# Newton steps of a Stieltjes attention: two-input operations to GpSimd, one-input sums on VectorE

## The chip, the cores and the metric

One Trainium2 chip; the kernel runs on one of its cores. A core has five engines that run their own instruction streams: TensorE (PE; its weight loads are listed apart as PEld), VectorE (DVE), ScalarE (ACT), GpSimd (POOL) and SyncE (SP, which here issues the transfers). They wait for each other through semaphores. SBUF is the working memory of 128 partitions, PSUM the memory that TensorE writes. The metric is the device time of one execution in microseconds (us), lower is better; times are medians over executions.

## The reference

The input x is 8 sequences of 512 tokens of width 128. There are two parts, each behind a layer norm.

**Part A** is one causal "Stieltjes" attention with 16 heads of 8 channels. With scores s of one query row, it looks for the number lam at which the sum over the allowed keys of 1 / (lam - s) is 1, by four Newton steps:

```python
lam = s_masked.max(-1) + 1.0
for _ in range(num_iter):                     # 4
    d = jnp.maximum(lam[..., None] - s, EPS)
    w = jnp.where(mask, d ** (-q), 0.0)       # q = 1
    f = w.sum(-1) - 1.0
    fp = -q * jnp.where(mask, d ** (-q - 1.0), 0.0).sum(-1)
    lam = lam - f / fp
```

The weights 1 / (lam - s), divided by their sum, then weigh the values, and an output projection and the residual follow.

**Part B** is six layers. Each has a local attention (16 heads of 64 channels, windows of 32 tokens that also see the window before) and a gated feed-forward. Queries and keys are divided by their norm, `t / max(norm(t), 1e-12)`, scaled and rotated; the feed-forward starts with a layer norm. Each works on x with half of its channels shifted by one token.

## The kernel before, in words

**Part A** works on batches: one sequence and four of the 16 heads at a time, so 32 batches. `project` (L198) fetches x, normalizes and transposes it (`normalized_T`, L176; the scaled subtraction of each 128x128 block is L188) and forms queries, keys and values. `mask_q` (L238) multiplies the 128x512 queries by a per-partition mask that leaves the heads of the batch. `scores` (L242) leaves minus the scores in SBUF (tile `ns`, four row blocks, each in four pieces whose lengths are 32 to 512 keys: 16 columns of row state altogether), and their minimum in `mn`. `first_lam` (L266) makes the opening value from the minimum. A Newton step is then made of:

- `add_lam` (L261, L264): for the two short row blocks GpSimd adds lam to the negated scores. For the two long ones ScalarE does that inside its logarithm (L281).
- `evaluate` (L272): ScalarE forms 1/d as exp(-ln d); VectorE takes the statistics of each piece by `bn_stats` (L284), which leaves a count, a mean and a sum of squared deviations for each of two halves of the piece, in the tile `st` (128 x 16 x 2 x 3).
- `step` (L286): from these 96 numbers per partition, seven VectorE instructions of 16 to 64 columns compute the sum of w, the sum of w squared, and the new lam (L290 to L299):

```python
nc.vector.tensor_tensor(s1, mean, st[:, :, :, 0], ALU.mult)
nc.vector.tensor_tensor(q2, s1, mean, ALU.mult)
nc.vector.tensor_reduce(sw2, st[:, :, :, 0:3:2], axis=AX.XY, op=ALU.add)
nc.vector.scalar_tensor_tensor(sw, s1[:, :, 0], -1.0, s1[:, :, 1], ALU.add, ALU.add)
nc.vector.reciprocal(sw2, sw2)
nc.vector.tensor_tensor(sw, sw, sw2, ALU.mult)
nc.vector.scalar_tensor_tensor(lam, sw, 0.0, lam, ALU.max, ALU.add)
```

While one batch makes its four steps, the one before is weighed and summed (`attend_weigh`, `attend_sum`, `attend_end`) and the next one's scores are made. `stieltjes` (L360) hands out this work in quarters of a step: 464 quarters for the 7 sequences of the main stream. One sequence runs in a second stream with pools of its own, beside the first five batches of the main one. When a sequence is done, `sequence_end` (L346) fetches x again into a tile `xb`, adds, and writes to a scratch tensor x2; `enter` (L438) fetches that, normalizes and transposes it for part B. All three fetches use the tile name `xb`, with two buffers.

**Part B** walks through 48 units (layer, sequence), each in 8 slots of a pair of heads, so 384 slots (loop at L870). In each slot, `prepare_qk` (L594), one quarter ahead, projects queries and keys for two row blocks (L599), squares them on ScalarE (L605), multiplies by the rotation tables on VectorE (`qr`, L608), sums the squares (L614), adds the halves on GpSimd (L616), clamps the 128x16 sums from below (L622), turns them into 1/norm on ScalarE (L623, L624) and scales on GpSimd (L627). `prepare_v` makes the values, `spread` moves them by transfers on SP's queue (L652 to L657). `turn` transposes (L665, copied by ScalarE at L670), `weigh` makes the scores and takes off the row maximum (L684 to L695), `exponentials`, `turn_weights`, `gather` (L719, L728), `turn_sums` and `leave` finish the attention some slots later. `feed_forward` (L759) is a generator that advances by one piece per slot (by four in the first two sequences); its layer norm scales four 128x128 blocks at L778.

Part B starts after five batches of part A. From then on the loop also advances part A, by 1.65 quarters per slot (L930 to L932), until part A is done; the last 40% of the slots have part B alone.

The program is written in a language layer that derives every semaphore wait from the tiles that an instruction reads and writes. It fixes each engine's order of instructions before the run, with the written order as the priority and its own estimate of when inputs are ready; so on an engine, instructions of both parts are interleaved and not always in written order. At run time each engine works through its list in order.

Of the kernel before, what the change touches and what calls it, by code (L numbers as in the profile page):

```python
# [9 lines left out]
F32 = mybir.dt.float32  # L10
BF16 = mybir.dt.bfloat16
AF = mybir.ActivationFunctionType
ALU = mybir.AluOpType
# [37 lines left out]
def tile_kernel(  # L51
# [112 lines left out]

    STEPS = 4 * NUM_ITER

    def streams(pools, bank1):

        ns_p, dp, tr, pj, sm = pools

        def fetch(src):
            xb = pj.tile([P, NT, D], F32, name="xb", bufs=2)
            nc.sync.dma_start(xb, src.rearrange("(c p) d -> p c d", p=P))
            return xb

        def normalized_T(xb, dst):  # L176
            st = sm.tile([P, NT, 6], F32, name="st")
            mv = sm.tile([P, NT, 2], F32, name="mv")
            for c in range(NT):
                nc.vector.bn_stats(st[:, c, :], xb[:, c, :])  # L180
                nc.vector.bn_aggr(mv[:, c, :], st[:, c, :])
            rstd = sm.tile([P, NT], F32, name="rstd")
            nc.scalar.activation(rstd, mv[:, :, 1], AF.Ln, bias=eps_ln)
            nc.scalar.activation(rstd, rstd, AF.Exp, scale=-0.5)
            xn = pj.tile([P, NT, D], F32, name="xn", tag="xn")
            pt = bank1([P, N], "pt")
            for c in range(NT):
                nc.vector.tensor_scalar(  # L188
                    xn[:, c, :], xb[:, c, :], mv[:, c, 0:1], rstd[:, c : c + 1],
                    ALU.subtract, ALU.mult,  # L190
                )
# [27 lines left out]
            )  # L219
            return qs, kn, va  # L220

        def keys(rb, a):
            return (rb + 1) * P - Q * (3 - a)
# [13 lines left out]

        def mask_q(t):  # L238
            t["qj"] = qj = pj.tile([P, N], F32, name="qj")
            nc.vector.tensor_scalar(qj, t["proj"][0], jmask[:, t["j"] : t["j"] + 1], None, ALU.mult)  # L240

        def scores(t, rb):  # L242
            kn, qj = t["proj"][1], t["qj"]
# [21 lines left out]

        def first_lam(t):  # L266
            lam, mn = t["lam"], t["mn"]
            nc.vector.tensor_scalar(lam, mn, -1.0, 1.0, ALU.mult, ALU.add)
            for e in (2.0**-21, -(2.0**-21)):
                nc.vector.scalar_tensor_tensor(lam, mn, -1.0 - e, lam, ALU.mult, ALU.max)  # L270

        def evaluate(t, rb):  # L272
            ns, lam = t["ns"][rb], t["lam"]
# [11 lines left out]

        def step(t):  # L286
            st, lam = t["st"], t["lam"]
            mean = st[:, :, :, 1]
            s1 = sm.tile([P, H, 2], F32, name="s1")
            nc.vector.tensor_tensor(s1, mean, st[:, :, :, 0], ALU.mult)  # L290
            q2 = st[:, :, :, 0]
            nc.vector.tensor_tensor(q2, s1, mean, ALU.mult)
            sw2 = sm.tile([P, H], F32, name="sw2")
            nc.vector.tensor_reduce(sw2, st[:, :, :, 0:3:2], axis=AX.XY, op=ALU.add)
            sw = sm.tile([P, H], F32, name="sw")
            nc.vector.scalar_tensor_tensor(sw, s1[:, :, 0], -1.0, s1[:, :, 1], ALU.add, ALU.add)
            nc.vector.reciprocal(sw2, sw2)
            nc.vector.tensor_tensor(sw, sw, sw2, ALU.mult)
            nc.vector.scalar_tensor_tensor(lam, sw, 0.0, lam, ALU.max, ALU.add)  # L299

        def attend_weigh(t, rb):
            d = t["ns"][rb]
# [57 lines left out]
        def stieltjes(seqs):  # L360

            work = [(b, j) for b in seqs for j in range(4)]
            state = {}

            def open_batch(w):
                b, j = work[w]
                if j == 0:
                    state["proj"] = project(b)
                    state["o"] = pj.tile([P, NT, H, DH], F32, name="o")
                t = batch(b, j, state["proj"], state["o"])  # L370
                mask_q(t)
                return t

            now = open_batch(0)
            for rb in (3, 2, 1, 0):
                scores(now, rb)
            before = None
            for w in range(len(work) + 1):
                nxt = None
                if now:  # L380
                    first_lam(now)
                for k in range(NUM_ITER):
                    if now:
                        now["st"] = sm.tile([P, H, 2, 3], F32, name="stw")
                        now["df"] = {}
                        for rb in (1, 0):
                            now["df"][rb] = d = dp.tile([P, width(rb)], F32, name=f"df{rb}", bufs=1)
# [12 lines left out]
                    if now:  # L400
                        evaluate(now, 2)
                    if before and k == 0:
                        attend_weigh(before, 3)
                    if k == 0 and w + 1 < len(work):
                        nxt = open_batch(w + 1)
                    yield
                    if now:
                        evaluate(now, 1)
                    if before and k in (1, 2):
                        attend_sum(before, 4 - k)  # L410
                    if before and k == 1:
# [12 lines left out]
                before, now = now, nxt  # L424
# [144 lines left out]
        nc.gpsimd.tensor_copy(xs[hf:D, 1:N], xT[b][hf:D, 0 : N - 1])  # L569
        return xs  # L570

    turns = {"n": 0}

    def bank(shape, name):
        if done_steps >= (4 * NB + 1) * STEPS:
# [8 lines left out]
    for v in vst:  # L584
        nc.gpsimd.memset(v.rearrange("p c e h d -> p (c e h) d")[:, :, DHL:], 1.0)

    marks = {"act": None}

    def begin(u, qt, xs):
# [4 lines left out]
    def prepare_qk(g, wqkv, tab, cs):  # L594
        xs, q0 = g["xs"], (g["qt"] % 2) * HQ * DHL
        ss = ep.tile([P, 2, 2 * HQ], F32, name="ss", bufs=3)
        for i, c in enumerate(cs):
            m = bank([P, 2, HQ, DHL], "m")
            nc.tensor.matmul(  # L599
                m.rearrange("p t h e -> p t (h e)"), lhsT=xs[:, c * P : (c + 1) * P],  # L600
                rhs=wqkv[:, 0:2, q0 : q0 + HQ * DHL], start=True, stop=True,
            )
            qr = ep.tile([P, 2, 2, HQ, DHL], F32, name="qr")
            sq = ep.tile([P, 2 * HQ, DHL], F32, name="sq", bufs=1)
            marks["act"] = nc.scalar.activation(  # L605
                sq, m.rearrange("p t h e -> p (t h) e"), AF.Square
            )
            nc.vector.tensor_tensor(  # L608
                qr, m.unsqueeze(1).to_broadcast([P, 2, 2, HQ, DHL]),
                tab[:, i].rearrange("p (k t) e -> p k t e", k=2).unsqueeze(3).to_broadcast(  # L610
                    [P, 2, 2, HQ, DHL]
                ), ALU.mult,
            )
            nc.vector.tensor_reduce(ss[:, i, :], sq, axis=AX.X, op=ALU.add)  # L614
            halves_of = qr.rearrange("p k t h (u e) -> p k (t h) u e", u=2)
            nc.gpsimd.tensor_tensor(  # L616
                g["qn"][:, c].rearrange("p t h (u e) -> p (t h) u e", u=2),
                halves_of[:, 0], halves_of[:, 1, :, ::-1, :], ALU.add,
            )
        gelus()  # L620

        nc.vector.tensor_scalar(ss, ss, 1e-24, None, ALU.max)  # L622
# [136 lines left out]
    def feed_forward(u, w1, w2):  # L759
# [15 lines left out]
        nc.scalar.activation(rn, mv[:, :, 1], AF.Ln, bias=eps_ln)  # L775
        nc.scalar.activation(rn, rn, AF.Exp, scale=-0.5)
        for c in range(NT):
            nc.vector.tensor_scalar(  # L778
                xt[:, c, :], xt[:, c, :], mv[:, c, 0:1], rn[:, c : c + 1],
                ALU.subtract, ALU.mult,  # L780
            )
# [202 lines left out]
```

## Time and profile before

| | |
|---|---|
| median of 3 executions | 4896.63 us (4894.68 to 4904.67) |
| profiled execution | 4896.56 us, span 4894.9 us |
| instructions | 165932 |
| PE busy | 4172.2 us (85%) |
| DVE busy | 4155.8 us (85%) |
| ACT busy | 3517.7 us (72%) |
| POOL busy | 2990.9 us (61%) |
| granted TensorE clock, mean | 0.938 |

The profile is of one execution, by the hardware's own records; the span is from its first to its last instruction. "L12" is line 12 of the kernel. A group is a set of instructions of one line and shape, with its count, its busy time and the mean duration of one (ns); then follows how long its engine sat idle just before, and on what. In the answer for a single line, three numbers stand for the minimum, median and maximum duration in ns. In a timeline each row gives the start, the duration, the engine, the line and what is written from what; equal neighbours are merged, with their count. A wait is given as the waiting engine and line, the releaser, the total us, how often, and the longest. In a table of stretches, each engine's busy time stands in the order PE, PEld, DVE, ACT, POOL, followed by the granted clock of TensorE, the DMA share and GB/s.

### The profile page before, as it was taken

What the parts mean: (1) busy time and instruction counts of PE and PEld (TensorE: products, weight loads), DVE (VectorE), ACT (ScalarE), POOL (GpSimd) and SP (SyncE); (2) the same over time, 40 slices, a digit from 0 to 9 for tenths busy, and PEclk for the clock granted to TensorE, in tenths of its full rate; (3) what the DMA queues carried; (4) which work ended last, traced back from release to release, by engine and by line L of the source; (5) the groups of instructions that cost most, each with busy time, mean ns of one, the idle gap of its engine ahead of it and who ended that gap; (6) DMA issues with size and microseconds to landing.
All of it is one profiled execution on the core that took longest, in us unless ns stands there. A gap on an engine that the chain in (4) does not pass through costs nothing. (4 is left out here: it accounts for less than half of the span.)

```text
span 4894.9 us, 165932 instructions
## 1 busy us (share of the span) xinstructions
PE 4172.2 (85%) x68749; PEld 2525.4 (52%) x68749; DVE 4155.8 (85%) x9460; ACT 3517.7 (72%) x6298; POOL 2990.9 (61%) x3822
## 2 busy tenths in 40 slices
PE   4555788888888888898888888888999999999998
PEld 1232455544555454554555555555566666666664
DVE  8787888988999989988889999898787777777775
ACT  6898777777777777766777777777566666666664
POOL 3543666656566655666666665666566666666763
PEclk7666899999999999999999999999999999999999
DMA  1000222222222222222222222222233333333332
GB/s 47 1 1 26 52 65 52 62 59 54 59 54 69 61 56 46 65 59 46 63 53 57 53 48 67 47 55 59 65 89 79 80 87 71 85 73 83 85 72 57
DMA packets 558914, 288.89 MB, mean 59 GB/s; under 512 B 97580, under 2 KB 541264, under 8 KB 558160
## 3 DMA queue, kind: packets, MB, share of 16 engines
q1 hardware_dynamic: 558160, 278.26, 24.4%
q8 instruction: 543, 8.90, 0.8%
q14 instruction: 211, 1.73, 0.1%
HBM read 66.21 MB, written 7.34 MB: 15 GB/s over the span
## 5 line engine op out<-in xcount | busy, mean ns | idle before, releaser
L616 POOL TENSOR_TENSOR qn<-qr 128x512 f32<-128x512 f32 x768 | 979.1, 1275 | 1157.1 <-DVE qr L608 1128.4
L608 DVE TENSOR_TENSOR qr<-m,tab 128x1024 f32<-128x1024 f32 x768 | 935.6, 1218 | 293.8 <-ACT sq L605 245.9
L627 POOL TENSOR_TENSOR qn<-qn,ss 128x512 f32<-128x512 f32 x768 | 785.5, 1043 | 113.5 <-ACT ss L624 91.4
L599 PE MATMUL m<-wqkv,xs 128*128 128x512 f32 x1536 | 767.4, 616 | 54.9 <-ACT qT L670 43.8
L281 ACT ACTIVATE d<-ns,lam 128x416 f32<-128x416 f32 (+7 forms) x1024 | 577.8, 623 | 138.4 <-DVE lam L299 103.2
L605 ACT ACTIVATE sq<-m 128x512 f32<-128x512 f32 x768 | 459.1, 598 | 261.9 <-DVE ss L614 180.6
L264 POOL TENSOR_TENSOR df<-ns,lam 128x160 f32<-128x160 f32 (+7 forms) x1024 | 400.6, 427 | 330.5 <-DVE lam L299 207.7
L284 DVE BATCH_NORM_STATS2 stw<-d 128x6 f32<-128x416 f32 (+7 forms) x1024 | 520.5, 561 | 95.7 <-ACT d L282 94.5
L670 ACT COPY qT<-ptq 128x512 f32<-128x512 f32 x768 | 426.4, 586 | 167.2 <-PE ptq L665 165.2
L614 DVE TENSOR_REDUCE ss<-sq 128x8 f32<-128x512 f32 x768 | 517.5, 674 | 0.0
L636 PE MATMUL pv<-wqkv,xs 128*128 128x256 f32 x1536 | 450.1, 416 | 58.4 <-DVE qr L608 43.7
L665 PEld LDWEIGHTS ptq<-ident,qn 128*128 128x128 f32 x3072 | 356.1, 143 | 255.7 <-issue 91.4
L665 PE MATMUL ptq<-ident,qn 128*128 128x128 f32 x3072 | 454.6, 282 | 38.7 <-ACT v L639 22.1
L695 POOL TENSOR_TENSOR pr<-pr,nm 128x512 f32<-128x512 f32 x384 | 400.2, 1042 | 68.7 <-DVE nm L694 57.0
L316 PE MATMUL dTp<-ident,ns 128*128 128x128 f32 x1280 | 245.4, 314 | 224.1 <-ACT ns L304 134.2
L740 ACT COPY oT<-po 128x512 f32<-128x512 f32 x384 | 224.5, 585 | 283.8 <-PE po L736 283.5
L252 PE MATMUL s<-kn,qj 32*32 32x224 f32 (+15 forms) x4096 | 365.7, 430 | 71.3 <-DVE mn L256 59.0
L744 PE MATMUL acc<-oT,wo 128*128 128x512 f32 x768 | 402.2, 606 | 2.7 <-ACT oT L740 2.7
L719 PE MATMUL po<-v,prT 64*32 64x65 f32 x24576 | 393.7, 226 | 6.8 <-DVE pr L689 6.6
L599 PEld LDWEIGHTS m<-wqkv,xs 128*128 128x128 f32 x1536 | 265.4, 197 | 255.2 <-issue 121.3
L282 ACT ACTIVATE d<-d 128x1856 f32<-128x1856 f32 (+1 forms) x256 | 393.0, 1535 | 0.0
L719 PEld LDWEIGHTS po<-v,prT 64*32 64x32 f32 x24576 | 289.8, 106 | 167.4 <-issue 107.2
(135 smaller groups left out, 8118.3 us busy)
## 6 DMA issues: line engine op xcount, KB each, us to landing
v<-v SPq DMA_DIRECT2D x2304, 65.0 KB
v<-v SPq DMA_DIRECT2D x768, 48.8 KB
wqkv<-in_L_ffn_Wqkv_dram SPq DMA_DIRECT2D x72, 256.0 KB
v<-v SPq DMA_DIRECT2D x384, 32.5 KB
wqkv<-in_L_ffn_Wqkv_dram SPq DMA_DIRECT2D x72, 128.0 KB
wo<-in_L_ffn_Wo_dram SPq DMA_DIRECT2D x36, 256.0 KB
tab<-tabs SPq DMA_DIRECT2D x36, 256.0 KB
w<-in_L_ffn_W_dram SPq DMA_DIRECT2D x18, 341.0 KB
```

Source lines behind the costliest of these rows:

```text
L281: nc.scalar.activation(o, n, AF.Ln, bias=lam[:, c : c + 1])
L284: nc.vector.bn_stats(t["st"][:, 4 * rb + a].rearrange("p u k -> p (u k)"), o)
L599: nc.tensor.matmul(m.rearrange("p t h e -> p t (h e)"), lhsT=xs[:, c * P : (c + 1) * P], rhs=wqkv[:, 0:2, q0 : q0 + HQ * DHL], start=True, ...
L605: marks["act"] = nc.scalar.activation(sq, m.rearrange("p t h e -> p (t h) e"), AF.Square)
L608: nc.vector.tensor_tensor(qr, m.unsqueeze(1).to_broadcast([P, 2, 2, HQ, DHL]), tab[:, i].rearrange("p (k t) e -> p k t e", k=2).unsqueeze( ...
L614: nc.vector.tensor_reduce(ss[:, i, :], sq, axis=AX.X, op=ALU.add)
L616: nc.gpsimd.tensor_tensor(g["qn"][:, c].rearrange("p t h (u e) -> p (t h) u e", u=2), halves_of[:, 0], halves_of[:, 1, :, ::-1, :], ALU.add,)
L627: nc.gpsimd.tensor_tensor(qc, qc, ss[:, i, :].unsqueeze(2).to_broadcast([P, 2 * HQ, DHL]), ALU.mult)
L636: nc.tensor.matmul(pv[:, i], lhsT=xs[:, c * P : (c + 1) * P], rhs=cols, start=True, stop=True,)
L665: nc.tensor.transpose(pt[:, c * P : (c + 1) * P], g["qn"][:, c, t, 2 * p : 2 * p + 2, :].rearrange("p h e -> p (h e)"), ident,)
L670: nc.scalar.copy(q, pt)
L719: nc.tensor.matmul(po[u * QB : (u + 1) * QB, e, c, :], lhsT=prT[rows, c, u * QB : (u + 1) * QB], rhs=g["v3"][rows, n, p, :], start=True, s ...
```

## The change

The four two-input operations of a Newton step go from VectorE to GpSimd. VectorE keeps two reductions over small extra axes in place of the sum with a constant and of the maximum, besides the reduction and the reciprocal that it had. The count from `bn_stats` is replaced by a constant tile `counts`; the -1 of "sum - 1" stands in a third column of `s1`, and the 0 of the maximum in a second column of `pos`, both in tiles that are filled once and used in turn. The opening value becomes three scaled copies on GpSimd and one maximum on VectorE. In part B the clamp of the norm sums becomes a maximum over pairs, whose second member is a constant 1e-24 in one of three tiles filled once. The query mask moves from VectorE to ScalarE. The scaled subtractions of both layer norms (L188, L778) move from VectorE to GpSimd. The fetch tile `xb` has one buffer instead of two.

```diff
+    counts = k1.tile([P, H, 2], F32, name="counts")
+    for rb in range(NT):
+        for a in range(4):
+            nc.gpsimd.memset(counts[:, 4 * rb + a], keys(rb, a) / 2)
...
+        sums = [sm.tile([P, H, 3], F32, name=f"sums{i}", bufs=1) for i in range(2)]
+        for s1 in sums:
+            nc.gpsimd.memset(s1, -1.0)
+        over = [sm.tile([P, H, 2], F32, name=f"over{i}", bufs=1) for i in range(2)]
+        for pos in over:
+            nc.gpsimd.memset(pos, 0.0)
+        state = {"n": 0}
...
-            xb = pj.tile([P, NT, D], F32, name="xb", bufs=2)
+            xb = pj.tile([P, NT, D], F32, name="xb")
...
-                nc.vector.tensor_scalar(
+                nc.gpsimd.tensor_scalar(
                     xn[:, c, :], xb[:, c, :], mv[:, c, 0:1], rstd[:, c : c + 1],
                     ALU.subtract, ALU.mult,
                 )
...
-            nc.vector.tensor_scalar(qj, t["proj"][0], jmask[:, t["j"] : t["j"] + 1], None, ALU.mult)
+            nc.scalar.activation(
+                qj, t["proj"][0], AF.Identity, scale=jmask[:, t["j"] : t["j"] + 1]
+            )
...
-            nc.vector.tensor_scalar(lam, mn, -1.0, 1.0, ALU.mult, ALU.add)
-            for e in (2.0**-21, -(2.0**-21)):
-                nc.vector.scalar_tensor_tensor(lam, mn, -1.0 - e, lam, ALU.mult, ALU.max)
+            least = sm.tile([P, H, 3], F32, name="least")
+            for i, (f, c) in enumerate(((-1.0, 1.0), (-1.0 - 2.0**-21, 0.0), (-1.0 + 2.0**-21, 0.0))):
+                nc.gpsimd.tensor_scalar(least[:, :, i], mn, f, c, ALU.mult, ALU.add)
+            nc.vector.tensor_reduce(lam, least, axis=AX.X, op=ALU.max)
...
             st, lam = t["st"], t["lam"]
+            state["n"] += 1
+            s1 = sums[state["n"] % 2]
             mean = st[:, :, :, 1]
-            s1 = sm.tile([P, H, 2], F32, name="s1")
-            nc.vector.tensor_tensor(s1, mean, st[:, :, :, 0], ALU.mult)
             q2 = st[:, :, :, 0]
-            nc.vector.tensor_tensor(q2, s1, mean, ALU.mult)
+            nc.gpsimd.tensor_tensor(s1[:, :, 0:2], mean, counts, ALU.mult)
+            nc.gpsimd.tensor_tensor(q2, s1[:, :, 0:2], mean, ALU.mult)
+            pos = over[state["n"] % 2]
+            nc.vector.tensor_reduce(pos[:, :, 0], s1, axis=AX.X, op=ALU.add)
+            sw = sm.tile([P, H], F32, name="sw")
+            nc.vector.tensor_reduce(sw, pos, axis=AX.X, op=ALU.max)
             sw2 = sm.tile([P, H], F32, name="sw2")
             nc.vector.tensor_reduce(sw2, st[:, :, :, 0:3:2], axis=AX.XY, op=ALU.add)
-            sw = sm.tile([P, H], F32, name="sw")
-            nc.vector.scalar_tensor_tensor(sw, s1[:, :, 0], -1.0, s1[:, :, 1], ALU.add, ALU.add)
             nc.vector.reciprocal(sw2, sw2)
-            nc.vector.tensor_tensor(sw, sw, sw2, ALU.mult)
-            nc.vector.scalar_tensor_tensor(lam, sw, 0.0, lam, ALU.max, ALU.add)
+            nc.gpsimd.tensor_tensor(sw2, sw2, sw, ALU.mult)
+            nc.gpsimd.tensor_tensor(lam, lam, sw2, ALU.add)
...
+    guarded = [k2.tile([P, 2, 2 * HQ, 2], F32, name=f"raw{i}") for i in range(3)]
+    for raw in guarded:
+        nc.gpsimd.memset(raw, 1e-24)
...
+        turns["s"] += 1
+        raw = guarded[turns["s"] % 3]
...
-            nc.vector.tensor_reduce(ss[:, i, :], sq, axis=AX.X, op=ALU.add)
+            nc.vector.tensor_reduce(raw[:, i, :, 0], sq, axis=AX.X, op=ALU.add)
...
-        nc.vector.tensor_scalar(ss, ss, 1e-24, None, ALU.max)
+        nc.vector.tensor_reduce(ss, raw, axis=AX.X, op=ALU.max)
...
         for c in range(NT):
-            nc.vector.tensor_scalar(
+            nc.gpsimd.tensor_scalar(
                 xt[:, c, :], xt[:, c, :], mv[:, c, 0:1], rn[:, c : c + 1],
                 ALU.subtract, ALU.mult,
             )
```

More of the change, by code (lines that the diff above doesn't have):

```diff
@@ L165, in tile_kernel, with keys @@
     STEPS = 4 * NUM_ITER
+    def keys(rb, a):
+        return (rb + 1) * P - Q * (3 - a)
+    counts = k1.tile([P, H, 2], F32, name="counts")
+    for rb in range(NT):
+        for a in range(4):
+            nc.gpsimd.memset(counts[:, 4 * rb + a], keys(rb, a) / 2)
     def streams(pools, bank1):
         ns_p, dp, tr, pj, sm = pools
+        sums = [sm.tile([P, H, 3], F32, name=f"sums{i}", bufs=1) for i in range(2)]
[5 more added lines that the diff above has]
+        state = {"n": 0}
         def fetch(src):
-            xb = pj.tile([P, NT, D], F32, name="xb", bufs=2)
+            xb = pj.tile([P, NT, D], F32, name="xb")
             nc.sync.dma_start(xb, src.rearrange("(c p) d -> p c d", p=P))
@@ L220, in project @@
             return qs, kn, va
-        def keys(rb, a):
-            return (rb + 1) * P - Q * (3 - a)
         def pieces(d, rb):
@@ L362, in stieltjes @@
             work = [(b, j) for b in seqs for j in range(4)]
-            state = {}
             def open_batch(w):
@@ L570, in shifted @@
         return xs
-    turns = {"n": 0}
+    turns = {"n": 0, "s": 0}
     def bank(shape, name):
```

## The prediction

> **What bounds the kernel now.** I read the page's first two parts first, then the stretches by stage, then groups by shape, single lines, a timeline and the waits.
>
> ```profile
> PE 4172.2 (85%) x68749; PEld 2525.4 (52%) x68749; DVE 4155.8 (85%) x9460; ACT 3517.7 (72%) x6298; POOL 2990.9 (61%) x3822
> ```
>
> PE and DVE tie over the whole span, so the mean says nothing; the busy times by stage do. Columns: stretch, its length, busy us of PE, PEld, DVE, ACT, POOL, then PE's granted clock.
>
> ```profile
> 40.00:490.00 450.00, 219.44 (x2046) 113.55 (x2045) 360.35 (x1283) 396.60 (x562) 187.84 (x411) 0.65 0.04 12
> 500.00:3440.00 2940.00, 2528.87 (x40745) 1504.15 (x40745) 2631.30 (x6116) 2207.24 (x3950) 1847.71 (x2416) 0.95 0.24 57
> 3440.00:4895.00 1455.00, 1391.23 (x25648) 892.06 (x25648) 1127.77 (x1910) 899.35 (x1762) 935.86 (x914) 0.99 0.34 77
> ```
>
> There are three stages. First the Stieltjes part alone: ACT 88%, DVE 80%. Then both parts mixed: DVE 89.5%, PE 86.0%. Last the second part alone: PE 95.6%, DVE 77.5%. The change acts on DVE, so the middle stage decides. Next, VectorE's groups by shape (count, then busy us and mean ns):
>
> ```profile
> L622 DVE TENSOR_SCALAR ss<-ss 128x16 f32<-128x16 f32 x384 | 141.8, 369 | 0.1
> L778 DVE TENSOR_SCALAR xt<-xt,mv,rn 128x128 f32<-128x128 f32 x192 | 86.7, 495 | 11.8 <-ACT rn L776 9.0 <-POOL qn L616 1.7 <-issue 1.0
> L296 DVE SCALAR_TENSOR_TENSOR sw<-s 128x16 f32<-128x16 f32 x128 | 56.5, 442 | 0.0
> L297 DVE RECIPROCAL sw<-sw 128x16 f32<-128x16 f32 x128 | 31.2, 244 | 0.9
> L294 DVE TENSOR_REDUCE sw<-stw 128x16 f32<-128x64 f32 x128 | 26.3, 205 | 0.0
> ```
>
> L296 handles 16 results and takes twice as long as L294, which reads 64 elements. The single lines (minimum/median/maximum ns) say why:
>
> ```profile
> L296 DVE SCALAR_TENSOR_TENSOR sw<-s x128: 140/169/2601, 57.4 to 3423.2; 128x16 f32<-128x16 f32 x128
> L294 DVE TENSOR_REDUCE sw<-stw x128: 160/206/221, 57.7 to 3423.4; 128x16 f32<-128x64 f32 x128
> L807 DVE SCALAR_TENSOR_TENSOR gate<-ap,vec,gate x144: 724/743/753, 691.4 to 4886.9; 128x512 f32<-128x512 f32 x96, 85x512 f32<-85x512 f32 x48
> ```
>
> Usually L296 is quick; sometimes it is held for over 2 us. A reduction never is, nor L807, whose first input lies in PSUM. What holds the others is on the timeline:
>
> ```profile
> 3427.81 7.86 POOL L264 TENSOR_TENSOR ns<-ns,lam 128x480 f32<-128x480 f32 x14
> ...
> 3434.97 4.18 DVE L622 TENSOR_SCALAR ss<-ss 128x16 f32<-128x16 f32 x1
> ...
> 3435.63 2.50 POOL L616 TENSOR_TENSOR qn<-qr 128x512 f32<-128x512 f32 x2
> ...
> 3438.08 1.04 POOL L695 TENSOR_TENSOR pr<-pr,nm 128x512 f32<-128x512 f32 x1
> ```
>
> A 16-element clamp ends at 3439.15, when GpSimd's unbroken run ends at 3439.12. So VectorE operations that work from SBUF with two inputs, or in the TENSOR_SCALAR form, sit until GpSimd pauses; reductions do not. Everything that the change takes off VectorE is of the held kind, everything that it leaves is not. GpSimd itself has room:
>
> ```profile
> POOL qn L616 <- DVE qr L608: 1128.4, 599, 11.6
> DVE qr L608 <- ACT sq L605: 245.9, 264, 4.1
> ```
>
> **The change part by part.** Durations on DVE overlap: its groups add up to 4754 us against 4155.8 busy, 598 over 9460 instructions, 0.06 us each; small ones start some 0.1 us apart with rows of 0.17 to 0.2. I take 0.09 us off each small instruction. The counts below are those of the mixed stage, from the stretches cut by line.
>
> Newton step, 92.5 in this stage. Before: seven VectorE instructions, L290 to L299, 224.5 us here, or 2.43 a step; less 7 x 0.09, 1.80. After: four. The sum over (mean, mean, -1) and the maximum over pairs read 48 and 32 elements: 0.19 and 0.175, between the 0.172 of the 16-to-4 reduction at L130 and L294's 0.205. With L294 and L297 (0.244) that is 0.81, less 0.36: 0.45. Saved 1.35 a step, 125 us.
>
> Opening value, 23: L268 and L270 took 42.3 us for 69 instructions, 36 after overlap; one reduction of 0.1 each is left: 34 saved. The query mask L240: 17.5 us for 22, 15 saved. Norms: L188 22.7 us (44) and L778 55.2 us (108) go to GpSimd: 19 and 45 saved. The clamp L622: 94.7 us for 226, 74 after overlap, becomes a pair reduction of 0.18 (0.09 net): 54 saved. Writing the norm sums with stride 2 at L614 I cost at nothing: no row shows a strided reduction output; the work is the 512 elements it reads (674 ns). If each cost 0.1 us more, it would take 45 us of the saving. Sum 292: DVE's 2631 becomes 2339.
>
> What GpSimd gets there: four operations a step, 0.24 each (its 128x32 addition at L264 takes 240 ns, so 16 columns not more), 0.93 a step, 86 us; three scalings per opening, 15; 152 norms. A 128x128 two-input addition there takes 398 ns, one 64x511 copy 612 ns, so a scaled subtraction of 128 columns lies between about 0.2 and 0.4; if its two per-row scalars are slow, twice that. I take 0.33, nearest to the row of the same size: 50. GpSimd goes from 1848 to 1999 us. ACT gets 22 masks, between 0.58 (L203's copy) and 0.79 (L787, the same function from PSUM); I take 0.7, 15 us.
>
> How much of 292 reaches the end? In full the stage would be 2648, with PE at 95.5% and DVE at 88.3%; no stage shows both. PE's and DVE's shares add up to 175.5% in the mixed stage and 173.1% in the last: whichever is the bound, the sum holds. At the mean, 174.3%, (2529 + 2339) / 1.743 gives 2793: a gain of 147, the figure I take. Ends: 0 (neither order nor PE lets it through) and 292.
>
> The new waits. VectorE's first sum waits for GpSimd's products, and GpSimd's last two for VectorE's reciprocal. Behind the waiting sum stand qr (L608), the norm sums (L614) and the scores (L689), for which GpSimd, PE and ACT wait. A crossing costs 0.08 us (L299 ends at 2036.97, L264 starts at 2037.05). With GpSimd free the step takes 0.24 + 0.08 + 0.19 + 0.175 + 0.2 + 0.24 + 0.08 + 2 x 0.24, less 0.3 overlap, 1.4 us; now it runs from 482.71 to 484.17, 1.46. With GpSimd busy (63%) on a 1.04 to 1.28 us operation, the mean rest is half of that, 0.6, so 0.38 at each of two entries. The two entries, 0.76, stand in place of today's holds, already counted; the part that no other VectorE work fills I put at 0.27 a step, a third: 25 us. Ends: 0 (the order written ahead puts other work between, as now: L728 runs between L290 and L292 at 2028.04) and 4 us a step, two L627 pairs of 2.04, 377.
>
> A rule speaks against this. The Trainium skill, GPSIMD Engine Reference, section 4.1, keeps elementwise work on VectorE, GpSimd being about twice as slow for two inputs. By that rule, at twice VectorE's medians, a step would take GpSimd 1.49 us, not 0.93, and if that lay wholly on the path 92 steps would add 52 us, to 4821. The rows at these sizes are nearer to each other: 240 ns there, 199 median and 340 mean here (L292).
>
> First stage, 36 steps: ACT binds it and gets ten masks, 7 us; its waits for the new value (22.7 on L299, 12.6 on L270) may shrink by as much or double. I take 0, ends -35 and +42. Last stage: PE binds it; the clamp (47 us) and the norms (32) leave a VectorE that has 327 us idle. I take -10, ends -64 (its whole distance from PE's busy 1391) and +20 (84 norms behind GpSimd's queue at 0.24).
>
> One input buffer instead of two: 24 fetches, behind the v transfers on SP's queue as now. VectorE waited 1.55 us and 1.94 us for two that follow each other near 500; one buffer puts them in line: +3, ends 0 and 24 x 2 = 48. The filling of the new tiles, 27 instructions of some 0.1 us on POOL, is hidden in its first 30 us, of which it works 11.6; uncovered 2.7.
>
> Sum: 4894.9 - 147 + 25 + 0 - 10 + 3 = 4765.9, and 1.7 us around the span (4896.56 against 4894.9): 4768. The profiled execution is 0.07 us off the median, 4896.63.
>
> **The rivals.** (a) It all comes through: 292 and no stall, -10: 4595. For it: VectorE's idle time in the mixed stage is only 309 us, and PE's clock is 0.95 there, 0.99 after it. Against: PE would need its last-stage share beside a VectorE at 88%.
> (b) Nothing comes through: the fixed order and PE's transposes keep the pace, 4895 give or take 10. For it: VectorE waits 97 us for ACT's squares in that stage. Against: waits for VectorE stand ahead of most others there.
> (c) Slower, by one mechanism: the Newton step and GpSimd's queue wait for each other in the mixed stage, since the step's products queue behind L627 pairs (2.04) and L264 runs (up to 7.86), and VectorE stands still at the first sum. Without any stall the sum is 4743, 154 below now, so it decides beyond 1.7 us a step (154 / 92.5). At 4 us: 4743 + 370 = 5113; at 2 us 4928. Against: GpSimd is idle 37% of the stage, and today's holds are of that size already.
>
> **How the numbers follow.** Forecast 0.50, its own range 4690 to 4850 (the share sum at 175.5% or 173.1% moves it by 20, the stall and the outer stages the rest); (a) 0.20, (b) 0.10, (c) 0.20. The range 4610 to 4925 holds the forecast, (b), two thirds of (a) and the mild third of (c), 0.8. A change under 0.2%, 10 us, can't be told from none. Faster: 0.50 + 0.20 + 0.04 of (b) = 0.74; same 0.06; slower 0.20.
>
> **What would show it.** Right: no VectorE instruction from SBUF over 0.3 us on the step's lines and the clamp; DVE near 2340 us in the mixed stage; that stage near 2820; GpSimd about 2000 there; the last stage within 20 us. Wrong: VectorE idle before the first sum with GpSimd as releaser, over 140 us; scaled subtractions on GpSimd over 0.7 us; PE's share in the mixed stage still 86%.

## The result, and the profile after

The changed kernel takes 4972.65 us (4969.56 to 4983.76), the kernel before 4895.68 us beside it: a ratio of 1.0165, interval 1.0148 to 1.0181. It is 77 us slower; 4768 was forecast, and the time lies above the range.

The page of the changed kernel shows what the change was to do, and that it did not pay. Engine, busy us, share of the span, instructions:

```profile
PE 4198.6 (84%) x68749; PEld 2552.7 (51%) x68749; DVE 3791.5 (76%) x8724; ACT 3540.9 (71%) x6330; POOL 3319.7 (67%) x4713
```

VectorE works 364 us less than before (4155.8), GpSimd 329 more (2990.9), and the kernel is longer. To compare stages by equal work I use the moment at which the attention of a unit is added to x (L924 before, L946 after, 48 times), read from the trace: first unit, 28th unit, last unit.

| | until the first | first to 28th (mixed stage) | 28th to last | last |
|---|---|---|---|---|
| before | 655.7 | 2826.8 | 1386.3 | 4868.8 |
| after | 689.1 | 2888.1 | 1367.3 | 4944.5 |
| difference | +33 | +61 | -19 | +76 |

The same mixed stage as a stretch of the trace, before and after (its ends here, and in the stretches further on, lie within 0.5 us of these moments). Columns: stretch, length, busy us of PE, PEld, DVE, ACT, POOL, then PE's clock.

```profile
655.70:3482.50 2826.80, 2443.55 (x39618) 1455.36 (x39599) 2522.34 (x5849) 2122.89 (x3789) 1760.62 (x2296) 0.96 0.24 57
```

```profile
689.30:3577.40 2888.10, 2472.42 (x39622) 1480.51 (x39612) 2252.58 (x5375) 2133.57 (x3808) 1955.66 (x2848) 0.94 0.23 55
```

VectorE is relieved of 270 us in it, and the stage is 61 us longer. VectorE's share falls from 89.2% to 78.0%, PE's from 86.4% to 85.6%. For the same matmuls PE is busy 29 us longer, at a granted clock of 0.94 instead of 0.96; whether that is a part of the loss or follows from the pauses isn't shown. The holds themselves are gone, as the lines of the changed kernel show (minimum/median/maximum ns):

```profile
L310 DVE TENSOR_REDUCE over<-sums x128: 152/202/205, 61.3 to 3516.7; 128x16 f32<-128x48 f32 x128
L644 DVE TENSOR_REDUCE ss<-raw x384: 127/176/188, 555.0 to 4908.3; 128x16 f32<-128x32 f32 x192
```

L310 stands in place of L296, whose maximum was 2601 ns; L644 in place of the clamp L622, whose maximum was 4180. What came instead stands in the waits of the changed kernel (waiter, releaser, total us, times, longest): VectorE for GpSimd's three scaled copies (L284) and for its products (L307), ScalarE for the new value (L317), TensorE for the norms (L800).

```profile
DVE lam L285 <- POOL least L284: 109.6, 27, 9.6
DVE over L310 <- POOL sums L307: 89.6, 70, 5.9
...
DVE sw L314 <- POOL stw L308: 9.8, 22, 1.2
```

```profile
ACT d L296 <- POOL lam L317: 192.4, 81, 6.8
...
ACT d L296 <- DVE lam L285: 43.5, 19, 5.9
```

```profile
PE pn L807 <- POOL xt L800: 49.4, 46, 5.5
```

In the kernel before, ScalarE's and PE's waits for the same things were shorter, and the first three waits didn't exist:

```profile
ACT d L281 <- DVE lam L299: 103.2, 51, 4.6
ACT d L281 <- DVE lam L270: 35.1, 8, 12.2
```

```profile
PE pn L785 <- DVE xt L778: 23.1, 11, 5.1
```

One Newton step in the timeline of the changed kernel shows the rendezvous:

```profile
2002.25 1.76 DVE L299 BATCH_NORM_STATS2 stw<-df 128x6 f32<-128x160 f32 x8
2003.93 0.68 DVE L337 TENSOR_TENSOR dT<-dTp,seen 128x512 f32<-128x512 f32 x1
2004.09 0.26 POOL L307 TENSOR_TENSOR sums<-stw,counts 128x32 f32<-128x32 f32 x1 [8.39 <-DVE stw L299]
...
2006.18 0.22 POOL L317 TENSOR_TENSOR lam<-lam,sw 128x16 f32<-128x16 f32 x1
...
2006.44 2.82 ACT L296 ACTIVATE d<-ns,lam 128x416 f32<-128x416 f32 x5 [0.16 <-POOL lam L317]
```

GpSimd stood 8.39 us before the products, with everything later in its list behind them, until VectorE's last statistics. Here, with GpSimd free, products to new value take 2.3 us, where 1.4 was estimated.

Last, the norms. On GpSimd they take 793 ns, where 0.33 us was assumed (column: count, busy us, mean ns):

```profile
L800 POOL TENSOR_SCALAR xt<-xt,mv,rn 128x128 f32<-128x128 f32 x192 | 149.8, 793 | 9.3 <-ACT rn L798 9.3
```

### The profile page after: what moved, and what is told of

Read it like the earlier page. It is cut to its first block, busy times and chain, and to the rows that moved or that the text cites. A ratio compares the mean times of both kernels' runs of the same rounds, so it can differ in the third digit from the quotient of the medians.

```text
span 4973.1 us, 166030 instructions
## 1 busy us (share of the span) xinstructions
PE 4198.6 (84%) x68749; PEld 2552.7 (51%) x68749; DVE 3791.5 (76%) x8724; ACT 3540.9 (71%) x6330; POOL 3319.7 (67%) x4713
## 5 line engine op out<-in xcount | busy, mean ns | idle before, releaser
L296 ACT ACTIVATE d<-ns,lam 128x416 f32<-128x416 f32 (+7 forms) x1024 | 580.9, 623 | 236.1 <-POOL lam L317 192.4
L636 DVE TENSOR_REDUCE raw<-sq 128x8 f32<-128x512 f32 x768 | 518.8, 675 | 0.0
L266 PE MATMUL s<-kn,qj 32*32 32x320 f32 (+15 forms) x4096 | 356.6, 433 | 64.5 <-DVE mn L270 46.8
```

The source lines that it names most:

```text
L296: nc.scalar.activation(o, n, AF.Ln, bias=lam[:, c : c + 1])
L636: nc.vector.tensor_reduce(raw[:, i, :, 0], sq, axis=AX.X, op=ALU.add)
```

## The experiments

All times are medians; ratios are against the kernel before, run beside each. The median of the kernel before lay between 4888.5 and 4896.8 us in these rounds, so a difference between runs of different rounds is good to some 8 us. Two theories at first: the crossings between VectorE and GpSimd cost more than the holds did (S for the step, L for the opening value), or the slow norms do (N).

### Undoing one part of the change at a time

The Newton step back on VectorE:

```diff
         def step(t):
...
-            nc.gpsimd.tensor_tensor(s1[:, :, 0:2], mean, counts, ALU.mult)
-            nc.gpsimd.tensor_tensor(q2, s1[:, :, 0:2], mean, ALU.mult)
...
-            nc.gpsimd.tensor_tensor(sw2, sw2, sw, ALU.mult)
-            nc.gpsimd.tensor_tensor(lam, lam, sw2, ALU.add)
+            nc.vector.tensor_tensor(s1, mean, st[:, :, :, 0], ALU.mult)
+            nc.vector.tensor_tensor(q2, s1, mean, ALU.mult)
...
+            nc.vector.tensor_tensor(sw, sw, sw2, ALU.mult)
+            nc.vector.scalar_tensor_tensor(lam, sw, 0.0, lam, ALU.max, ALU.add)
```

> The changed kernel with the Newton step back on VectorE alone (seven instructions); the rest of the change stays. Theory S (the step's crossings cost: VectorE stood 89.6 us before the first sum, GpSimd 222.3 us before the products): 4895 to 4925. Theory L (the opening value is the cost) and theory N (the norms on GpSimd are the cost): within 15 us of 4973, or above it, since VectorE's holds of 2.4 us a step come back in the mixed stage.

Measured 4899.91, ratio 1.0013 (1.0003 to 1.0024): 73 us of 77 come back, all but one twentieth. Until the first unit it is 17 us quicker than the changed kernel, in the mixed stage 54.

The opening value back on VectorE:

```diff
...
-                nc.gpsimd.tensor_scalar(least[:, :, i], mn, f, c, ALU.mult, ALU.add)
-            nc.vector.tensor_reduce(lam, least, axis=AX.X, op=ALU.max)
+            nc.vector.tensor_scalar(lam, mn, -1.0, 1.0, ALU.mult, ALU.add)
+            for e in (2.0**-21, -(2.0**-21)):
+                nc.vector.scalar_tensor_tensor(lam, mn, -1.0 - e, lam, ALU.mult, ALU.max)
```

> The changed kernel with the opening value back on VectorE (three instructions). Theory L (VectorE stood 109.6 us in 27 waits before the maximum over the three copies, in order, with all else behind it): 4880 to 4925. Theories S and N: within 15 us of 4973.

Measured 4934.73, ratio 1.0085 (1.0066 to 1.0105): 38 us back for 32 opening values, 43 of them in the mixed stage and 3 lost before. So 1.2 us apiece, net of the holds that return; less than theory L had, more than the others.

Both norms back on VectorE:

```diff
-                nc.gpsimd.tensor_scalar(
+                nc.vector.tensor_scalar(
                     xn[:, c, :], xb[:, c, :], mv[:, c, 0:1], rstd[:, c : c + 1],
...
-            nc.gpsimd.tensor_scalar(
+            nc.vector.tensor_scalar(
                 xt[:, c, :], xt[:, c, :], mv[:, c, 0:1], rn[:, c : c + 1],
```

> The changed kernel with both layer norms' scaled subtractions back on VectorE. Theory N (0.79 us each on GpSimd instead of the 0.33 I assumed, and TensorE waits 49.4 + 32.9 us for them): 4885 to 4930. Theories S and L: within 15 us of 4973.

Measured 4950.20, ratio 1.0116 (1.0097 to 1.0136): 22 us back, again between the theories' ranges. It has two sides: 11 us until the first unit and 32 in the mixed stage come back, but in the last stage 22 are lost (1388.9 against 1367.3). The last stage's gain in the changed kernel is the norms'.

Each of the three undone alone gives time back, so no single theory is right by itself. All three diffs together, so that the clamp, the mask and the fetch buffer stay:

> The changed kernel with the step, the opening value and both norms back on VectorE; the clamp, the mask on ScalarE and the one fetch buffer stay. Undoing them one by one gave 73, 38 and 22 us. If these add: 4973 - 133 = 4840, give or take 10. If they were costly only together, so that each undoing gave the same time back: 4870 or more.

Measured 4849.03, ratio 0.9912 (0.9890 to 0.9933), 9 us from the sum. The losses add, and what is left of the change is faster than the kernel before.

### Parts alone

One fetch buffer alone, as a base, since the added tiles of the other runs leave no room in SBUF for the second:

```diff
-            xb = pj.tile([P, NT, D], F32, name="xb", bufs=2)
+            xb = pj.tile([P, NT, D], F32, name="xb")
```

> The kernel before with one fetch buffer instead of two and nothing else. It is the base of the three runs beside it, and shows how far a change that removes and adds no work moves the time through the order of the instructions. I forecast +3 us: 4890 to 4905. If the order alone can move it by more, as much as 20 us either way.

Measured 4899.13, ratio 1.0016 (1.0004 to 1.0028). About 8 us.

The clamp as a maximum over pairs, and one fetch buffer:

```diff
-            nc.vector.tensor_reduce(ss[:, i, :], sq, axis=AX.X, op=ALU.add)
+            nc.vector.tensor_reduce(raw[:, i, :, 0], sq, axis=AX.X, op=ALU.add)
...
-        nc.vector.tensor_scalar(ss, ss, 1e-24, None, ALU.max)
+        nc.vector.tensor_reduce(ss, raw, axis=AX.X, op=ALU.max)
```

> The kernel before with the clamp as a maximum over pairs and one fetch buffer, nothing else of the change. If VectorE's holds cost what the forecast's share rule says (54 us off VectorE in the mixed stage, half of it passed on, and some of the last stage's gain of 19 us): 4850 to 4880. If holds of a small instruction are hidden (rival b): 4890 to 4905. If the one fetch buffer is the cost: above 4910.

Measured 4845.30, ratio 0.9893 (0.9870 to 0.9916): 54 us under the run with one buffer alone, somewhat more than was expected. The profiled execution is the quickest of its four (4830.68): 63 us under the profiled one with one buffer alone, 52 of these in the mixed stage. Its stretch there:

```profile
648.40:3415.20 2766.80, 2420.90 (x39605) 1445.86 (x39583) 2467.47 (x5836) 2122.00 (x3787) 1760.08 (x2296) 0.97 0.25 58
```

VectorE has 55 us less to do than before (2522), and the stage is 60 us shorter: all or, at the median time, most of it came through, where half was allowed. The strided output of the sums cost nothing that shows: that line's mean is 674 ns, as before.

The new step alone, and its two crossings apart. In the first of the three runs the whole step is as in the change; in the second only the products are on GpSimd, in the third only the last two operations. The diffs of the second and the third are against the first:

```diff
-            nc.gpsimd.tensor_tensor(sw2, sw2, sw, ALU.mult)
-            nc.gpsimd.tensor_tensor(lam, lam, sw2, ALU.add)
+            nc.vector.tensor_tensor(sw2, sw2, sw, ALU.mult)
+            nc.vector.tensor_tensor(lam, lam, sw2, ALU.add)
```

```diff
-            nc.gpsimd.tensor_tensor(s1[:, :, 0:2], mean, counts, ALU.mult)
-            nc.gpsimd.tensor_tensor(q2, s1[:, :, 0:2], mean, ALU.mult)
+            nc.vector.tensor_tensor(s1[:, :, 0:2], mean, counts, ALU.mult)
+            nc.vector.tensor_tensor(q2, s1[:, :, 0:2], mean, ALU.mult)
```

> The kernel before with one fetch buffer and the new Newton step, nothing else. Undoing the step in the changed kernel gave 73 us back. Theory S (the step's crossings cost by themselves): 4945 to 4985. If it costs only together with the slow norms and the opening value on GpSimd (a full GpSimd queue): 4890 to 4925.

Measured 4933.08, ratio 1.0086 (1.0062 to 1.0110): 34 us above one buffer alone, between the two ranges. The step loses by itself, but less than the 73 that it costs beside the norms and the opening value on GpSimd. Most of that is in the first stage: 24 us until the first unit, 16 in the mixed stage. The new work on GpSimd does not hold the rest of VectorE longer: outside the step, the durations of its instructions in the mixed stage add up to 2717 us, against 2709 with one buffer alone.

> As the run with the new step alone, but only the two products are on GpSimd; the last multiplication and the addition stay on VectorE, the two small sums as in the change. Theory F (the cost is VectorE standing at the first sum, behind GpSimd's queue): all of the new step's loss, within 15 us of that run. Theory K (the cost is the late new value, which ScalarE's logarithms wait for): within 15 us of the run with one fetch buffer.

Measured 4918.35, ratio 1.0054 (1.0037 to 1.0072).

> As the run with the new step alone, but only the last multiplication and the addition are on GpSimd; both products are on VectorE. Theory F: within 15 us of the run with one fetch buffer. Theory K: most of the new step's loss, 30 us or more above the run with one fetch buffer.

Measured 4919.44, ratio 1.0062 (1.0042 to 1.0083). Theory F's bound for the first run is just met (14.7 us under the new step alone), for the second it is missed; theory K fails in both. Each crossing costs its own 20 us, net of the holds that it removes, and the two make up the whole: 19 and 20 against 34.

### What the relief is worth without a crossing

The step cut to four one-input instructions on VectorE, with no GpSimd in it (lam isn't the root):

```diff
         def step(t):
...
+            nc.vector.tensor_reduce(pos[:, :, 0], s1, axis=AX.X, op=ALU.add)
+            nc.vector.tensor_reduce(sw, pos, axis=AX.X, op=ALU.max)
+            nc.vector.tensor_reduce(lam, st[:, :, :, 0:3:2], axis=AX.XY, op=ALU.add)
+            nc.vector.reciprocal(sw2, lam)
```

> The kernel before with one fetch buffer, and a Newton step cut down to the four one-input VectorE instructions that the change leaves there; the two products, the last multiplication and the addition are left out, so lam isn't the root. It bounds from above what freeing VectorE of the step's held instructions can give when no crossing is paid. Forecast's share rule (half of 125 us in the mixed stage passed on, some more in the first): 4820 to 4850. If the step's holds lie in slack and only the crossings counted: 4885 to 4905, as the run with one fetch buffer alone (4899).

Measured 4779.63, ratio 0.9777 (0.9762 to 0.9791): 119 us under one buffer alone, better than both ranges. That gain mixes fewer instructions, a shorter chain and no holds. It also goes further than was meant: without the products the two small sums wait for nothing, and the trace has all of them between 12.3 and 149.8 us, ahead of their steps. What runs in a step is two VectorE instructions, not four. So the next run keeps count and depth and takes away only the second inputs (the diff is against the run above; lam isn't the root here either):

```diff
+            nc.vector.tensor_reduce(pos[:, :, 0], st[:, :, :, 0:3:2], axis=AX.XY, op=ALU.add)
+            nc.vector.tensor_reduce(sw, pos, axis=AX.X, op=ALU.max)
+            nc.vector.reciprocal(sw2, sw)
+            nc.vector.reciprocal(two[:, :, 0], sw2)
+            nc.vector.tensor_reduce(sw2, two, axis=AX.X, op=ALU.max)
+            nc.vector.reciprocal(sw2, sw2)
+            nc.vector.reciprocal(lam, sw2)
```

> As the run with the reduced step, but with seven one-input VectorE instructions in one chain, as many as the step before and one deeper; lam isn't the root. No instruction of it has a second input in SBUF. Theory H (the 119 us that the reduced step gained are the holds of the two-input instructions): 4790 to 4825, three instructions of some 0.15 to 0.2 us each on 128 steps above the reduced step's 4780. Theory C (they are the smaller count and the shorter chain to the new value): 4860 to 4905.

Measured 4812.42, ratio 0.9831 (0.9809 to 0.9852): 87 us under one buffer alone, as theory H said (91 by the two ratios). Seven instructions without a second SBUF input are worth 87 us against seven of which five have one: I read that as the price of the five holds in the step. The stretches of the mixed stage, by equal work, for one buffer alone, for the reduced step, the seven, and the new step:

```profile
656.00:3475.10 2819.10, 2438.01 (x39618) 1458.52 (x39595) 2518.40 (x5838) 2122.69 (x3787) 1760.34 (x2297) 0.96 0.24 57
```

```profile
650.20:3361.00 2710.80, 2413.37 (x39588) 1454.82 (x39587) 2383.86 (x5398) 2126.66 (x3788) 1758.52 (x2297) 0.96 0.25 59
```

```profile
638.10:3391.00 2752.90, 2422.54 (x39602) 1450.60 (x39603) 2445.74 (x5837) 2122.81 (x3793) 1759.90 (x2297) 0.96 0.25 58
```

```profile
679.60:3514.80 2835.20, 2438.39 (x39647) 1463.97 (x39647) 2410.74 (x5574) 2124.90 (x3787) 1842.25 (x2648) 0.96 0.24 56
```

PE's and DVE's shares add up to 175.8%, 177.0%, 176.8%, and with the crossings 171.0%. VectorE has 108 us less to do with the new step than with one buffer alone, and it all turns into waiting.

### The norms' length, and versions that keep what pays

Constants in place of mean and 1/deviation on GpSimd (nothing is normalized):

```diff
-                    xt[:, c, :], xt[:, c, :], mv[:, c, 0:1], rn[:, c : c + 1],
+                    xt[:, c, :], xt[:, c, :], 0.0, 0.01,
```

> The changed kernel with constants in place of the mean and of 1/deviation in both norms on GpSimd; so nothing is normalized. If the two per-row scalars make these 0.79 us long, they fall to 0.25 to 0.4 us. If that length is what undoing the norms gave back (22 us): 4940 to 4955 and the mixed stage gets shorter while the last one keeps its gain. If the move itself is the cost, whatever the length: 4965 to 4980.

Measured 4939.64, ratio 1.0103 (1.0088 to 1.0118). The line took 644 ns:

```profile
L800 POOL TENSOR_SCALAR xt<-xt x192: 637/644/652, 695.8 to 4922.8; 128x128 f32<-128x128 f32 x192
```

So the two per-row scalars are only 0.15 us of the 0.79; the form itself is slow. Yet the mixed stage is as short as with both norms on VectorE (2859.9 against 2856.4), with the last stage's gain kept (1369.9). The total lies 0.4 us under the range given for the length as the cause; the line is far from the 0.25 to 0.4 us expected. The run also takes away the wait for the statistics, so length and wait aren't told apart.

The clamp, one buffer, and the feed-forward norm on GpSimd only once part A is done:

```diff
+        scale = nc.gpsimd if done_steps >= total else nc.vector
         for c in range(NT):
-            nc.vector.tensor_scalar(
+            scale.tensor_scalar(
```

> The clamp as a maximum over pairs, one fetch buffer, and the feed-forward norm on GpSimd only for the units after part A is done (the norm of the changed kernel went with 68.3 us per unit in the last stage, against 69.3 without it). If the parts add: 4845 less 17 to 20: 4820 to 4832. If the last stage's gain came from something else in the change: 4840 to 4850.

Measured 4818.70, ratio 0.9860 (0.9842 to 0.9878). It beats both kernels; the last stage is 1368.6 against 1387.7 with the clamp alone. The same with the query mask on ScalarE:

```diff
-            nc.vector.tensor_scalar(qj, t["proj"][0], jmask[:, t["j"] : t["j"] + 1], None, ALU.mult)
+            nc.scalar.activation(qj, t["proj"][0], AF.Identity, scale=jmask[:, t["j"] : t["j"] + 1])
```

> As the run beside it, with the query mask on ScalarE too. VectorE loses 23 us of work, ScalarE gets about as much. If VectorE's load in the mixed stage is what counts (share rule): 8 to 12 us faster than the run beside it. If only work that another engine waits for counts (nobody was seen waiting for the mask): within 6 us of it.

Measured 4823.61, ratio 0.9865 (0.9850 to 0.9880): no difference from the run beside it that can be told. The mask is worth nothing.

Two more attempts on the holds without a crossing, both on top of the fastest version. First, the step's statistics in PSUM, so that no instruction of it has two SBUF inputs, paid with one of part B's PSUM banks (`at` is a slice of a tile of `ps_s`):

```diff
-    ps_a = ctx.enter_context(tc.tile_pool(name="ps_a", bufs=3, space=PSUM))
+    ps_a = ctx.enter_context(tc.tile_pool(name="ps_a", bufs=2, space=PSUM))
+    ps_s = ctx.enter_context(tc.tile_pool(name="ps_s", bufs=1, space=PSUM))
...
-                        now["st"] = sm.tile([P, H, 2, 3], F32, name="stw")
+                        now["st"] = at[:, 0:96].rearrange("p (h u k) -> p h u k", h=H, u=2)
+                        now["root"] = at[:, 96 : 96 + H]
```

> The run with the clamp and the last stage's norms (4819), with the whole Newton step on VectorE and its statistics, squares and quotient in PSUM, so that each two-input instruction has one input in PSUM; the bank for it is taken from part B (two instead of three in its first group). Theory H: the holds go, without a crossing: 4819 less about 100 = 4700 to 4750 if the bank costs nothing; part B's transposes and projections may lose some of it for want of the bank, up to 100 in all, then about 4820. Theory C: no gain from the step, 4810 or more.

Measured 5408.50, ratio 1.1050 (1.1033 to 1.1067). Of 590 us, 413 are in the last stage, which has no step in it (1781.3 against 1368.6): the bank costs far more than was allowed. The holds did go. The multiplication that was held up to 1360 ns before, first as it was (L298), then in this run:

```profile
L298 DVE TENSOR_TENSOR sw<-sw,sw x128: 153/174/1360, 58.6 to 3423.9; 128x16 f32<-128x16 f32 x128
```

```profile
L315 DVE TENSOR_TENSOR stps<-stps,sw x128: 158/177/183, 66.9 to 3538.7; 128x16 f32<-128x16 f32 x128
```

Second, the two-input instructions cut from five to three:

```diff
-            nc.vector.scalar_tensor_tensor(sw, s1[:, :, 0], -1.0, s1[:, :, 1], ALU.add, ALU.add)
+            nc.vector.tensor_reduce(pos[:, :, 0], s1, axis=AX.X, op=ALU.add)
+            nc.vector.tensor_reduce(sw, pos, axis=AX.X, op=ALU.max)
...
-            nc.vector.tensor_tensor(sw, sw, sw2, ALU.mult)
-            nc.vector.scalar_tensor_tensor(lam, sw, 0.0, lam, ALU.max, ALU.add)
+            nc.vector.tensor_tensor(pair[:, :, 1], sw, sw2, ALU.mult)
+            nc.vector.tensor_reduce(t["lam"], pair, axis=AX.X, op=ALU.add)
```

> The run with the clamp and the last stage's norms (4819), with a Newton step wholly on VectorE in which the five two-input instructions are three: the sum with -1 and the maximum are the change's two reductions, and the last addition is a sum over pairs of the old value and the correction. Theory H (the holds of two-input instructions cost, 87 us in the chain of seven against the step before): two of five holds gone, the longest among them (442 ns mean), less one more instruction of 0.2 us: 4785 to 4805. If the count of instructions matters as much as the holds: 4815 to 4830.

Measured 4813.68, ratio 0.9839 (0.9820 to 0.9858): not to be told from the 0.9860 without it, a miss. The three that stay are held as before:

```profile
L302 DVE TENSOR_TENSOR stw<-sums,stw 128x32 f32<-128x32 f32 x128 | 44.8, 350 | 0.7
...
L301 DVE TENSOR_TENSOR sums<-stw 128x32 f32<-128x32 f32 x128 | 43.6, 341 | 0.4
L310 DVE TENSOR_TENSOR lam<-sw,sw 128x16 f32<-128x16 f32 x128 | 40.9, 320 | 0.9
```

In the kernel before these three had 340, 311 and 323 ns. Two held instructions became three that aren't; VectorE works 21 us less in the mixed stage (2444.3 against 2465.4), that stage is 8 us shorter, and the start 12 us later. So the 87 us can't be shared out by hold: with two of five gone, little or nothing came.

## Why the prediction was wrong

**The reading of the profile held.** What is held are VectorE's instructions with two SBUF inputs and its TENSOR_SCALAR forms from SBUF: a chain as long without them is 87 us faster, and with one input in PSUM the same multiplication takes 183 ns at most.

**VectorE's relief was sized rightly.** 292 us were forecast for the mixed stage, 270 are gone over its 27 units. The clamp's 55 us less on VectorE were 60 us of stage in its profiled execution, and the reduced step gave back 108 us of stage for 135 us less work. That half of it passes on was too careful for these two. The share rule itself holds where nothing crosses to GpSimd (175.7% to 177.0% over five kernels, the one before among them; I estimate that spread at 20 us of stage), and fails where something does: 171.0% with the new step alone, 163.6% with the whole change. The rule had no term for that.

**The step that failed is "the part that no other VectorE work fills I put at 0.27 a step, a third: 25 us".** It is the mechanism of the rival (c), mild, and not only at the place that (c) names. The new step against the seven-instruction chain without holds is 4933 - 4812 = 121 us, 0.94 us a step over 128 steps. In the profiled executions 82 us of it lie in the mixed stage (2835.2 against 2752.9, 88 steps), where 25 were put down, and 41 until the first unit, where nothing was. Against the reduced step it is 153 us, 1.2 a step, an upper bound, since only two instructions are left in that run's steps. The term took a third of VectorE's two rests, 0.76 us. VectorE stood 67.6 us before the first sum in the run with the new step alone, 89.6 in the changed kernel (0.7 a step; (c) named over 140 as its sign). But the stall isn't VectorE's alone: ScalarE waits for the new value too. Its waits with the seven, with one buffer alone and with the new step alone, then VectorE's in the last of these:

```profile
ACT d L288 <- DVE lam L305: 57.6, 31, 5.0
```

```profile
ACT d L282 <- DVE lam L300: 103.5, 51, 4.8
```

```profile
ACT d L293 <- POOL lam L314: 153.5, 75, 4.8
```

```profile
DVE over L307 <- POOL sums L304: 67.6, 61, 2.9
```

GpSimd's 222.3 us before the products are not a loss beside these: before, it stood 251.8 us ahead of its additions (L264) for the same chain's new value. A term for one engine was put where two stand. Beside the other new work on GpSimd the loss grows: 34 us alone, 73 in the whole change.

**The first stage was put at 0, and is 33 us longer.** Undoing the step gives 17 of that back, undoing the norms 11. The estimate that a step takes 1.4 us with GpSimd free, like now, took GpSimd to be free, and took one step of 1.46 us as typical. From the first product to the end of the new value, the steps that begin between 40 and 490 us take 2.52 us before and 3.32 after, on average; the other stream's additions share GpSimd there, but how much of the 0.80 us is theirs wasn't measured. In the mixed stage the same span got shorter, 4.95 to 3.87 us: the step itself is not slower there. What is lost there lies around it, in who stands while it is done.

**The opening value's crossing was left out.** 34 us were booked as saved and nothing as a wait; VectorE stands 109.6 us there, and undoing it gives 38 back.

**The norms were mis-sized**, 0.79 instead of 0.33 us; the upper bound in the text, twice 0.2 to 0.4, was the right one. In the mixed stage they cost 32 us, in the first 11. The last stage went better than forecast, -19 instead of -10, and that is the norms: the only run with them back on VectorE that keeps the rest has 1388.9 there, and the clamp alone, from which a gain was expected too, leaves it at 1387.7.

**The rule of the Trainium skill** (GPSIMD Engine Reference, section 4.1), that elementwise work stays on VectorE, was the better advice for the step. But its reason, a factor of about two for two inputs, is not what decided: priced by it, the prediction still came to 4821, below the kernel before, and at these sizes GpSimd's 256 ns (L307) stand against VectorE's median of 198 before (L290). The factor is stated for two inputs; the norms have one, and took 793 ns against a median of 341.

**The small terms**: the fetch buffer +3 forecast, about 8 measured (2 to 14 by its interval); the mask -7 in the sum (half of 15 saved), nothing that can be told.

Still open is how the loss of a crossing divides between engines standing in their fixed order and that order being planned anew: every edit moves all of it, and no run holds the order still. The run with one buffer alone, which changes no work, moved by 8 us, so differences of that size are read as nothing here.

## What to carry to other kernels

Price a chain that is moved between two in-order engines by the rendezvous, for every engine that waits for its result, not by the instruction times: here the two crossings of a Newton step cost 0.94 us against a chain without holds, and the holds that they were to avoid 0.68 (87 us over 128 steps). Take a hold away with a form that stays on its engine, as the pair reduction did, and first where another engine waits for that very instruction: the clamp, for which ScalarE stood 187.1 us, paid; the mask, for which TensorE's weight loads stood 1.0 us, did not. A sum of two engines' shares is a fair guide to what a relief gives only as long as no new wait comes with it.

## What the runs showed of the hardware that was not expected

GpSimd takes 793 ns for a TENSOR_SCALAR with two per-row scalars over 128 columns and 644 ns with two constants, but 398 ns for a two-input addition of the same size: the form is the slow part, the scalars add 0.15 us. And one PSUM bank fewer for part B, three to two in its first group, made its units in the last stage 89.1 us long instead of 68.4.
